# Layer 0 of a four-layer network: the position bias as three half-size Toeplitz products in place of four, and the residual copied to phase order by ScalarE

## The chip, the cores and the metric

The kernel runs on one core of a Trainium2 chip. Its time is the device time of one execution in microseconds (us); the figure compared is the median over runs. A profile is one execution of the same program taken by the hardware profiler. PE is TensorE's matmul, PEld its weight load, DVE is VectorE, ACT is ScalarE, POOL is GpSimd, SP is SyncE, which here only issues DMAs.

## What is computed

The input x is float32 of shape (T=4, B=8, N=512, D=512). Four layers follow one another, each of the form x = x + layer(groupnorm(x)). Layer 0 is a spiking attention; layers 1 to 3 are convolutions, which the change doesn't touch. Cut to what matters:

```python
# layer 0, on the group-normed x; lif() is a leaky neuron over the time axis T that gives 0/1 spikes
q = heads(lif(bn(x @ Wq.T)))          # H = 8 heads of 64
k = heads(lif(bn(x @ Wk.T)))
v = heads(lif(bn(x @ Wv.T)))
scores = einsum('tbhnd,tbhmd->tbhnm', q, k) / sqrt(D)
rel = pos[None, :] - pos[:, None] + (N - 1)
scores = scores + bias_table[rel].transpose(2, 0, 1)   # depends on m - n and the head alone
out = lif(einsum('tbhnm,tbhmd->tbhnd', scores, v))
out = lif(bn((out * gate_scale + gate_shift) @ Wp.T))
x = x + out
# layers 1 to 3: x = x + conv(groupnorm(x))
```

There is no softmax, so the attention falls into two linear parts: q (k^T v) / sqrt(D), and a product of v with a bias matrix that is Toeplitz (constant along its diagonals) for each head.

## The kernel before, in words

The program is written with a tile framework. It fixes the order of instructions on each engine when the program is built: a planner with its own estimates of durations takes the instructions in the order in which they are written as priorities, starts what it takes to be ready, and gives out the buffers. `tc.issue_after` adds an order by hand. On the chip each engine works through its list in that fixed order, and waits where its data or buffer is not there yet.

Layer 0 runs over 32 steps, a batch element b and a time t each (`steps`, t innermost). In one turn of the main loop stands, in this order:

- `attend` for step n: k^T v for pairs of heads (L540), masked to the diagonal blocks by DVE into kvb (L545); then for each of the four pairs of heads j the product of q with it into the PSUM tile pa (L552, one buffer), and the bias product into pb (L560, two buffers). The bias table is held as three bf16 parts (z) in the tiles `toep`, reversed so that a slice of 512 columns is the moving operand for a chunk c of 128 tokens. So a step has 4 pairs x 4 chunks x 3 parts x 2 heads = 96 matmuls of 512 columns. The two heads of a pair write the two halves of the PSUM partitions. DVE then adds pa and the neuron's state (L572; ScalarE does it for t = 0, L570), adds pb (L575), makes the spikes `so` (L469), and resets (L471); ScalarE halves the state (L473).
- `load_x` of the residual xr (SyncE, L438), from the pool `x0` of six buffers, shared with the loads xs for the statistics of the next group of batch elements (L456).
- `project_in` for step n + 1: v, k and q, each in four chunks of eight PE instructions (L524), their potentials and spikes on DVE (L485, L492, L529, L469, L499, L471), the states of v and k on GpSimd (L500), that of q on ScalarE (L475). vtok, k and q have one buffer each.
- Between those, `project_out` of step n: four chunks (L587). The potential v_p comes out in phase order (every fourth column together), as layer 1 wants it. DVE adds the spikes to the residual (L598, two instructions of 256 elements in a chunk, reading xr at a stride of four elements) into x1s, a tile with two buffers, and takes its statistics (L602). GpSimd copies mirrored edges (L609) and stores the tile (L614). ScalarE issues six DMAs for mirrored rows where the chunk is the first or the last (L617, L620).
- In between, DVE normalises the input of step n + 2 (L643) and transposes it in four pieces into xn (L505, six buffers), which all projections of that step read.

At the start the bias table is loaded, split in three parts by DVE and stored to DRAM (`split_bias`, L369 to L375). Then `prepare_bias` loads each pair of heads of each part as 128 shifted rows (hankel, L388; 2 x 896 columns, 448 KB) and ScalarE copies it reversed into `toep` (L394), twelve times.

Layer 1 (L843) and layers 2 and 3 (L1146, L1249) follow. Constants of the later layers (`same`, `ind`, `mask2`) are loaded with `block` in one DMA at the start (L142).

Of the kernel before, what the change touches and what calls it, by code (L numbers as in the profile page):

```python
# [129 lines left out]
def network(ctx: ExitStack, tc: tile.TileContext, i: dict, out: bass.AP):  # L130
# [9 lines left out]
    n_c = i["c128"].shape[1] - SHIFTS * M1  # L140
    c128 = const.tile([P, n_c], F32, name="c128")
    nc.gpsimd.dma_start(c128, i["c128"][:, :n_c])  # L142
    at = 0

    def part(n):
        nonlocal at
        at += n
        return c128[:, at - n : at]

    block, same, ind = part(P), part(P), part(G)  # L150
    mask2 = part(W2_N * 2)
# [8 lines left out]
    avg_same = const.tile([P, P], F32, name="avg_same")  # L160
# [49 lines left out]
    st1 = [const.tile([P, T, PAIR, NC, 2, 6], F32, name=f"st1_{g}") for g in range(G)]  # L210
# [20 lines left out]
    nc.vector.tensor_scalar_mul(avg_same, same, 1.0 / n_half)  # L231

# [3 lines left out]
    late = ctx.enter_context(pool("late", side="right"))  # L236
    st2 = late.tile([P, T, B, W1_N // 2 // N_PS1, 6], F32, name="st2")
# [30 lines left out]
def layer0(  # L268
# [22 lines left out]
    toep = [wpool.tile([P, H, NC * P + N - P], BF16, name=f"toep_{j}") for j in range(3)]  # L291
# [5 lines left out]
    xp = s.enter_context(tc.tile_pool(name="x0", bufs=6))  # L297
# [32 lines left out]
    def as_rows_of(cols):  # L330

        n = cols.shape[1]
        ps = ps_mm.tile([n, P], F32, tag="mm", name="ps_rows")
        nc.tensor.transpose(ps, cols, ident)
        rows = wpool.tile([4 * NC, P], F32, tag="rows", name="rows", bufs=2)
        nc.scalar.copy(rows[:n], ps)
        return rows[:n]
# [16 lines left out]

    def prepare_in(n):
# [6 lines left out]
    n_h, n_u = 2 * N - 1, toep[0].shape[2]  # L362

    def split_bias():

        n_e = n_h // 3
        parts = tc.dram_tile([3, H * n_h], BF16, name="bias_parts")
        src = state.tile([3 * H, n_e], F32, tag="h_o", name="bias_table")
        nc.scalar.dma_start(src, bass.AP(i["table"].tensor, 0, [[n_e, 3 * H], [1, n_e]]))  # L369
        part = state.tile([3 * H, 3, n_e], BF16, tag="h_p", name="bias_part")  # L370
        for z in range(3):
            nc.vector.tensor_copy(part[:, z, :], src)
            if z < 2:
                nc.vector.tensor_sub(src, src, part[:, z, :])
        nc.scalar.dma_start(  # L375
            bass.AP(parts.tensor, parts.offset, [[n_e, 3 * H], [H * n_h, 3], [1, n_e]]), part
        )
        return parts

    def prepare_bias(parts):  # L380


        for h in range(0, H, 2):
            for z in range(3):
                hankel = state.tile(
                    [P, 2, n_u], BF16, tag="h_o" if (h + z) % 2 else "h_p", name="hankel"
# [4 lines left out]
                        parts.tensor, parts.offset + (z * H + h) * n_h, [[1, P], [n_h, 2], [1, n_u]]  # L391
                    ),
                )
                nc.scalar.copy(toep[z][:, h : h + 2, :], hankel[:, :, ::-1])  # L394
# [6 lines left out]
    def prepare_out(wp32):  # L401
# [3 lines left out]
        for e in range(NC):  # L405
# [16 lines left out]
            c_twice["p"].rearrange("p (g v) -> p g v", g=PH), phases(along_free(as_rows_of(c), 0)), 2.0  # L422
        )
        for k in range(NC):
            wp = work.tile([P, D], F32, tag="v", name="wp_k", bufs=3)
            nc.vector.scalar_tensor_tensor(
                wp.rearrange("p (g v) -> p g v", g=PH), phases(wp32[:, k, :]),
# [14 lines left out]
    def load_quarters(b, t):  # L442
# [5 lines left out]
        return xt  # L448

# [52 lines left out]
    def transposed(xt, k):  # L502

        xk = work.tile([P, N], F32, tag="xn", name="xn", bufs=6)
# [28 lines left out]
    def attend(got, t):  # L533
# [13 lines left out]
        for j in range(NC):  # L547
            pa = ps_1.tile([P, N], F32, tag="pa", name="ps_a")
            pb = ps_b.tile([P, N], F32, tag="pb", name="ps_b")
            for two in range(2):  # L550
                out = slice(two * DH, (two + 1) * DH)
                nc.tensor.matmul(  # L552
                    pa[out, :], lhsT=kvb[:, j, out], rhs=q[:, j, :], start=True, stop=True
                )
            for c in range(NC):
                u = P * (NC - 1 - c)
                for z in range(3):
                    for two in range(2):
                        h = 2 * j + two
                        nc.tensor.matmul(  # L560
                            pb[two * DH : (two + 1) * DH, :],
                            lhsT=v[:, c, h * DH : (h + 1) * DH],
                            rhs=toep[z][:, h, u : u + N],
                            start=c == 0 and z == 0,
                            stop=c == NC - 1 and z == 2,
                        )
            h = h_of["o"][:, j, :]
            w = work.tile([P, N], F32, tag="v", name="v_o", bufs=3)
            if t == 0:
                nc.scalar.mul(w, pa, half_scale)  # L570
            else:
                nc.vector.scalar_tensor_tensor(  # L572
                    w, pa, half_scale, h, op0=ALU.mult, op1=ALU.add
                )
            nc.vector.scalar_tensor_tensor(w, pb, 0.5, w, op0=ALU.mult, op1=ALU.add)  # L575
# [3 lines left out]
    def project_out(so, c, xt, b, t):  # L579
# [12 lines left out]
        x1 = x1p.tile([P, PH, X1_U], F32, tag="x1", name=f"x1s_{b}_{t}_{c}")  # L592
        by_phase = xt.rearrange("p (v g) -> p g v", g=PH)
        for z in range(2):
            f, u = (2 * z + R1) % PH, (2 * z + R1) // PH
            own = x1[:, f : f + 2, u : u + NV]
            two = slice(2 * z, 2 * z + 2)
            nc.vector.scalar_tensor_tensor(  # L598
                own, v.rearrange("p (g v) -> p g v", g=PH)[:, two, :], 1.0,
# [748 lines left out]
```

## Time and profile before

| | us |
|---|---|
| median of 3 runs | 2902.83 |
| lowest, highest | 2902.46, 2903.03 |
| profiled execution, span of the core's instructions | 2900.8 |
| the same with what lies around the span | about 2902.8 |
| start until the first projection (L524) | 22.7 |
| layer 0's steps, up to | about 2024 |
| layer 1, from / layers 2 and 3, from | 2032 / 2490 |

The page of a profile gives each engine's busy time and share, the span in slices, the DMA queues, the chain of work that ended last (followed back from the last instruction, at each step to what released it), and the costliest groups of instructions. A group's line reads: source line, engine, operation, output tile <- input tiles, shapes, count, then busy time and mean ns of one, then the idle time of the engine just before and what ended it. The busy time counts overlapping instructions once, so two matmuls that run side by side add less than their sum. In a timeline each line gives start and length in us, engine, line and operation; a length runs to the end of the instruction's own pipeline, so that neighbours overlap a little. The mean granted clock of TensorE was 0.991 of full speed over the span, 1.00 in layer 0 after its start, 0.91 in the first 110 us.

### The profile page before, as it was taken

Reading aid. Unit: us, or ns where it says so; the run is one execution under the profiler, and the core shown is the slowest. Engines: PE = TensorE matmul, PEld = TensorE weight load, DVE = VectorE, ACT = ScalarE, POOL = GpSimd, SP = SyncE. Lnnn points to the kernel's source line nnn. Section 1 sums busy time; section 2 is a strip of 40 time slices with the busy share of each in tenths; the row PEclk is TensorE's granted clock in tenths of the full one; section 3 lists DMA queues with packets and bytes.
Section 4 is the critical chain, followed back from the end, with each engine's and each line's share of the span. In section 5 each row is a group of like instructions: output and inputs, shape, how many; then the busy total and the mean of one; then the engine's idle time right before and its main releaser. Section 6 shows DMA issues by size and latency. Waiting matters only on the chain. (4 is left out here: it accounts for less than half of the span.)

```text
span 2900.8 us, 36559 instructions
## 1 busy us (share of the span) xinstructions
PE 2818.8 (97%) x12868; PEld 1302.5 (45%) x12868; DVE 2183.1 (75%) x3888; ACT 549.2 (19%) x851; POOL 868.8 (30%) x1920
## 2 busy tenths in 40 slices
PE   7999999999999999999999999999999999689999
PEld 3444555545555545455555555445333333223334
DVE  6897788788779878878877886886665665888870
ACT  2200100011010001001000000110111121677774
POOL 2242243333234323333422343332311111232220
PEclk9899999999999999999999999999999999999999
DMA  8433222223222232222222122212877788699975
GB/s 209 115 89 76 59 67 67 74 74 74 59 67 67 77 76 68 59 67 67 75 67 51 45 59 52 52 45 75 221 203 207 209 219 224 157 201 234 224 191 148
DMA packets 326127, 324.01 MB, mean 112 GB/s; under 512 B 21519, under 2 KB 240439, under 8 KB 325831
## 3 DMA queue, kind: packets, MB, share of 16 engines
q1 hardware_dynamic: 263024, 239.48, 34.1%
q0 software_dynamic: 19776, 56.14, 6.0%
q10 hardware_dynamic: 43143, 26.05, 3.1%
q8 instruction: 101, 1.65, 0.3%
q14 instruction: 83, 0.68, 0.1%
HBM read 212.44 MB, written 103.65 MB: 109 GB/s over the span
## 5 line engine op out<-in xcount | busy, mean ns | idle before, releaser
L524 PE MATMUL ps_in<-w_v,xn 128*128 128x512 f32 x1024 | 459.1, 599 | 5.4 <-DVE w_v L359 5.4
L524 PE MATMUL ps_in<-w_kq,xn 128*128 128x512 f32 x1024 | 449.8, 592 | 0.0
L843 PE MATMUL ps_conv<-x,bt 112*64 112x512 f32 x2048 | 445.2, 592 | 0.1
L524 PE MATMUL ps_in<-xn,w_kq 128*128 128x512 f32 x1024 | 444.9, 592 | 0.0
L560 PE MATMUL ps_b<-toep,vtok 128*64 128x512 bf16 x3072 | 367.1, 383 | 0.4 <-DVE v_o L575 0.4
L475 ACT ACTIVATE h_q<-v_q,c_half 128x512 f32<-128x512 f32 x96 | 69.1, 721 | 1473.6 <-DVE v_q L471 893.9
L500 POOL TENSOR_TENSOR h_v<-h_v,c_v 128x512 f32<-128x512 f32 x96 | 121.8, 1269 | 728.0 <-DVE h_v L499 700.1
L587 PE MATMUL ps_out<-wp,so 128*128 128x512 f32 x1024 | 308.7, 444 | 0.0
L609 POOL COPY x1s<-x1s 128x2 f32<-128x2 f32 (+1 forms) x1024 | 226.6, 275 | 273.0 <-DVE x1s L598 273.0
L524 PEld LDWEIGHTS ps_in<-xn,w_kq 128*128 128x128 f32 x1024 | 194.3, 190 | 232.5 <-issue 220.4
L524 PEld LDWEIGHTS ps_in<-w_kq,xn 128*128 128x128 f32 x1024 | 194.3, 190 | 220.7 <-issue 206.2
L524 PEld LDWEIGHTS ps_in<-w_v,xn 128*128 128x128 f32 x1024 | 191.4, 191 | 222.9 <-issue 212.1
L843 PEld LDWEIGHTS ps_conv<-x,bt 112*64 112x64 f32 x2048 | 146.5, 135 | 288.0 <-issue 286.0
L560 PEld LDWEIGHTS <-vtok 128*64 128x64 bf16 x3072 | 176.1, 111 | 155.1 <-issue 5.6
L1249 PE MATMUL ps_conv<-x,band_t 64*64 64x512 f32 x2040 | 242.7, 595 | 0.0
L587 PEld LDWEIGHTS ps_out<-wp,so 128*128 128x128 f32 x1024 | 192.6, 188 | 94.0 <-issue 57.8
L1153 DVE SCALAR_TENSOR_TENSOR x<-ps_conv,inv,x 128x512 f32<-128x512 f32 (+1 forms) x172 | 186.1, 1169 | 46.9 <-PE ps_conv L1146 46.7
L598 DVE SCALAR_TENSOR_TENSOR x1s<-v_p,xr 128x256 f32<-128x256 f32 x256 | 187.6, 773 | 14.6 <-DMA x<-x1s 3.8
L865 POOL DMA_DIRECT2D x<-xo x128 | 71.4, 564 | 330.6 <-ACT xo L850 316.3
L850 ACT ACTIVATE xo<-ps_conv,off 128x512 f32<-128x512 f32 x128 | 87.6, 687 | 430.6 <-PE ps_conv L843 307.4
L500 POOL TENSOR_TENSOR h_k<-h_k,c_k 128x512 f32<-128x512 f32 x96 | 122.0, 1270 | 138.4 <-DVE h_k L499 138.4
L1146 PE MATMUL ps_conv<-xq,band 128*128 128x512 bf16 (+1 forms) x516 | 131.5, 391 | 31.3 <-POOL xq L1129 31.3
(193 smaller groups left out, 3113.8 us busy)
## 6 DMA issues: line engine op xcount, KB each, us to landing
x<-x SPq DMA_DIRECT2D x64, 917.0 KB
x<-x SPq DMA_DIRECT2D x168, 256.0 KB
x<-x1s POOLq DMA_DIRECT2D x128, 262.0 KB, 2.7
xq<-in_x SPq DMA_DIRECT2D x128, 256.0 KB
xr<-in_x SPq DMA_DIRECT2D x128, 256.0 KB
out<-o SPq DMA_DIRECT2D x164, 192.0 KB
xs<-in_x SPq DMA_DIRECT2D x112, 256.0 KB
x<-xo ACTq DMA_DIRECT2D x128, 128.0 KB
```

Source lines behind the costliest of these rows:

```text
L500: nc.gpsimd.tensor_add(h, h, c_twice[n])
L524: mm = nc.tensor.matmul(ps, lhsT=lhsT, rhs=rhs, start=k == 0, stop=k == NC - 1)
L560: nc.tensor.matmul(pb[two * DH : (two + 1) * DH, :], lhsT=v[:, c, h * DH : (h + 1) * DH], rhs=toep[z][:, h, u : u + N], start=c == 0 and z ...
L587: nc.tensor.matmul(ps, lhsT=so[:, k, c * P : (c + 1) * P], rhs=wpT[z][:, k, :], start=k == 0 and z == 0, stop=k == NC - 1 and z == 1,)
L598: nc.vector.scalar_tensor_tensor(own, v.rearrange("p (g v) -> p g v", g=PH)[:, two, :], 1.0, by_phase[:, two, :], op0=ALU.is_ge, op1=ALU.add,)
L609: nc.gpsimd.tensor_copy(x1[:, f, u : u + n], x1[:, fm, um - n + 1 : um + 1][:, ::-1])
L843: mm = nc.tensor.matmul(ps[q * M1 : (q + 1) * M1, :], lhsT=bt[:, z, :], rhs=xt[:, w0 : w0 + N_PS1, z : z + NV], start=z == 0, stop=z == SH ...
L850: nc.scalar.activation(xo[:, a, :], ps, AF.Identity, bias=off[:, t : t + 1])
L865: engine.dma_start(bass.AP(dst.tensor, dst.offset + (q * n_half * W1_OUT * B + b) * D + f * NV, [[B * D, W1_OUT], [W1_OUT * B * D, n_half] ...
L1146: mm = nc.tensor.matmul(ps[:n_p, :], lhsT=w["band2"][:n_p, j, dx, :n_p], rhs=xq[:, j, dx : dx + PH, :], start=dx == 0, stop=dx == 2,)
L1153: done["DVE"] = nc.vector.scalar_tensor_tensor(own.rearrange("p (v g) -> p g v", g=PH), by_phase(ps[:n_p, :]), w["inv"][:n_p], by_phase(x[ ...
L1249: mm = nc.tensor.matmul(ps[j][b * HALF : (b + 1) * HALF, :], lhsT=band[half, b, dx, :], rhs=x3[half, s0 + j, dx : dx + D], start=dx == 0, ...
```

## The change

The 512 x 512 bias matrix of a head is seen as four blocks of 256 x 256: T0 on the diagonal (both blocks are the same), T+ and T- off it. With v's halves a (first 256 tokens) and b (last 256), the first half of the output is T0 (a + b) + (T+ - T0) b, the second half T0 (a + b) + (T- - T0) a. Three half-size products stand in place of four.

- `toep` holds for each head three tables of 384 columns (x = 0: T0; 1 and 2: the two differences) for one of 896. The bias table is scaled by sqrt(D) when it is prepared, so that q's product and the difference products add up in one PSUM tile pb (with `start=False` for the later ones); pa holds 256 columns of T0 (a + b), which both halves of the output read. The matmuls: 4 pairs x 3 products x 2 chunks x 3 parts x 2 heads = 144 of 256 columns.
- GpSimd makes `both` = a + b, bf16, 128 x 1024 elements a step. Its tile takes the one buffer of k.
- Preparation: five loads of the table for one, a subtraction and a scaling more on DVE, three stores for one; each hankel load is 6 x 384 columns (576 KB), as is each ScalarE copy.
- The residual: after its load ScalarE copies it in phase order into x1s (two copies of 256 elements a chunk); DVE's L598 then adds the spikes in place, reading contiguously. The x1s tile is now taken when the residual is copied.
- Room: `x0` has four buffers for six, xn five for six; the statistics tiles st1 of groups 2 and 3 are those of groups 0 and 1; the constants of the later layers are loaded after layer 0; two small tiles share the place of kvb.

```diff
-    toep = [wpool.tile([P, H, NC * P + N - P], BF16, name=f"toep_{j}") for j in range(3)]
+    toep = [wpool.tile([P, H, 3, N // 2 + P], BF16, name=f"toep_{j}") for j in range(3)]
-    xp = s.enter_context(tc.tile_pool(name="x0", bufs=6))
+    xp = s.enter_context(tc.tile_pool(name="x0", bufs=4))
...
-        for z in range(3):
-            nc.vector.tensor_copy(part[:, z, :], src)
-            if z < 2:
-                nc.vector.tensor_sub(src, src, part[:, z, :])
+        for x, first in enumerate((1, 2, 0)):
+            cut = slice(x * H, (x + 1) * H)
+            nc.scalar.dma_start(own[cut], rows(first))
+            if x > 0:
+                nc.scalar.dma_start(same[cut], rows(1))
+        nc.vector.tensor_sub(own, own, same)
+        nc.vector.tensor_scalar_mul(own, own, math.sqrt(D))
...
+    def own_of(x1, z):
+        f, u = (2 * z + R1) % PH, (2 * z + R1) // PH
+        return x1[:, f : f + 2, u : u + NV]
+
+    def residual_of(b, t):
+        got = []
+        for c, xt in enumerate(load_x(b, t, "xr")):
+            x1 = x1p.tile([P, PH, X1_U], F32, tag="x1", name=f"x1s_{b}_{t}_{c}")
+            for z in range(2):
+                nc.scalar.copy(own_of(x1, z), phases(xt)[:, 2 * z : 2 * z + 2, :])
+            got.append(x1)
+        return got
...
-        xk = work.tile([P, N], F32, tag="xn", name="xn", bufs=6)
+        xk = work.tile([P, N], F32, tag="xn", name="xn", bufs=5)
...
-        for j in range(NC):
-            pa = ps_1.tile([P, N], F32, tag="pa", name="ps_a")
-            pb = ps_b.tile([P, N], F32, tag="pb", name="ps_b")
-            for two in range(2):
-                out = slice(two * DH, (two + 1) * DH)
-                nc.tensor.matmul(
-                    pa[out, :], lhsT=kvb[:, j, out], rhs=q[:, j, :], start=True, stop=True
-                )
-            for c in range(NC):
-                u = P * (NC - 1 - c)
+        both = work.tile([P, NC, D], BF16, tag="k", name="both")[:, :2, :]
+        nc.gpsimd.tensor_add(both, v[:, :2, :], v[:, 2:, :])
+        half = N // 2
+
+        def biased(out, own, j, x):
+            for c in range(2):
+                u = P * (1 - c)
                 for z in range(3):
                     for two in range(2):
                         h = 2 * j + two
                         nc.tensor.matmul(
-                            pb[two * DH : (two + 1) * DH, :],
-                            lhsT=v[:, c, h * DH : (h + 1) * DH],
-                            rhs=toep[z][:, h, u : u + N],
-                            start=c == 0 and z == 0,
-                            stop=c == NC - 1 and z == 2,
+                            out[two * DH : (two + 1) * DH, :],
+                            lhsT=own[:, c, h * DH : (h + 1) * DH],
+                            rhs=toep[z][:, h, x, u : u + half],
+                            start=x < 2 and c == 0 and z == 0, stop=x == 0 and c == 1 and z == 2,
+                            skip_group_check=x > 0,
                         )
+
+        for j in range(NC):
+            pa = ps_1.tile([P, half], F32, tag="pa", name="ps_a")
+            pb = ps_b.tile([P, N], F32, tag="pb", name="ps_b")
+            biased(pb[:, :half], v[:, 2:, :], j, 1)
+            biased(pb[:, half:], v[:, :2, :], j, 2)
+            for two in range(2):
+                out = slice(two * DH, (two + 1) * DH)
+                nc.tensor.matmul(
+                    pb[out, :], lhsT=kvb[:, j, out], rhs=q[:, j, :], start=False, stop=True,
+                    skip_group_check=True,
+                )
+            biased(pa, both, j, 0)
...
-            residual = load_x(b, t, "xr")
+            residual = residual_of(b, t)
```

## The prediction

> **What bounds the kernel now.** I read the page's engine line and its costliest groups first, then the busy time by stretches of the span, then the chain of work that ended last, then the timeline around one step's attention. The page says that TensorE is busy almost throughout, and in which lines:
>
> ```profile
> PE 2818.8 (97%) x12868; PEld 1302.5 (45%) x12868; DVE 2183.1 (75%) x3888; ACT 549.2 (19%) x851; POOL 868.8 (30%) x1920
> L560 PE MATMUL ps_b<-toep,vtok 128*64 128x512 bf16 x3072 | 367.1, 383 | 0.4 <-DVE v_o L575 0.4
> L598 DVE SCALAR_TENSOR_TENSOR x1s<-v_p,xr 128x256 f32<-128x256 f32 x256 | 187.6, 773 | 14.6 <-DMA x<-x1s 3.8
> ```
>
> An average says little about the stage that is changed, so here are 31 of layer 0's 32 steps, and one step alone (columns: stretch, then its length and the busy time of PE, PEld, DVE, ACT, POOL):
>
> ```profile
> 110.00:2024.00 1914.00, 1904.11 (x7739) 962.26 (x7740) 1540.74 (x2578) 140.29 (x212) 657.05 (x1413) 1.00 0.25 66
> 1903.00:1964.00 61.00, 60.89 (x248) 30.69 (x248) 55.19 (x82) 5.41 (x8) 25.12 (x48) 1.00 0.11 36
> ```
>
> PE idles 1914.00 - 1904.11 = 9.9 us there, 0.32 us a step. Layer 0 is PE-bound at full granted clock, and a column taken from PE is worth its whole time until something else is late. DVE is next: 55.2 of 61.0 us. The rates of PE come from the chain, where the numbers are start and length:
>
> ```profile
> 1955.12 2.59 PE ps_b L560 x24
> ...
> 2012.16 0.89 PE ps_kv L540 x16
> ...
> 2102.26 1.04 PE ps_band L951 x32
> ```
>
> 24 bias matmuls of 512 columns take 2.59 us: 107.9 ns each, since the two heads of a pair run side by side in the two column halves. 16 matmuls of 128 columns, each with its own weight load, take 55.6 ns each. 32 small ones in column halves, each with its weight load, take 32.5 ns. So a weight load and a matmul every 54 ns is within what PE does here. Last, the hand-over between the q projection and the attention, in PE's and in DVE's order, and an earlier moment of the same step:
>
> ```profile
> 1950.62 1.06 PE L540 MATMUL ps_kv<-vtok,k 128*128 128x128 bf16 x16
> 1951.61 1.05 PE L560 MATMUL ps_b<-toep,vtok 128*64 128x512 bf16 x8
> 1952.77 0.41 PE L552 MATMUL ps_a<-q,kvb 128*64 128x512 f16 x2
> ```
>
> ```profile
> 1950.91 0.75 DVE L485 SCALAR_TENSOR_TENSOR v_q<-ps_in,a_half,h_q 128x512 f32<-128x512 f32 x1 [0.49 <-PE ps_in L524]
> 1951.69 0.43 DVE L469 TENSOR_SCALAR q<-v_q 128x512 f16<-128x512 f32 x1
> 1952.03 0.68 DVE L545 TENSOR_TENSOR kvb<-ps_kv,c 128x512 f16<-128x512 f32 x1
> ```
>
> ```profile
> 1942.43 1.92 DVE L469 TENSOR_SCALAR q<-v_q 128x512 f16<-128x512 f32 x1
> ```
>
> ```profile
> 1942.78 1.28 POOL L500 TENSOR_TENSOR h_p<-h_p,c_p 128x512 f32<-128x512 f32 x1
> ```
>
> The planner filled the wait for kvb with eight bias matmuls; they end at 1951.61 + 8 x 0.108 = 1952.47, and PE then waits 0.30 us, to 1952.77, about all of a step's idle time. The last two rows show a price that I need: the q spikes, 0.43 us when undisturbed, took 1.92 us when GpSimd's add fell upon them.
>
> **What the Trainium skill says.** "SBUF — State Buffer", Who interferes with whom: VectorE and GpSimd share a port pair; a VectorE operation in a two-port mode and a GpSimd instruction exclude each other for their whole length, and a VectorE operation with two SBUF inputs excludes a GpSimd reader. The 1.92 us row agrees. "GPSIMD Engine Reference", 3.1 Elementwise: a two-input add costs about 2.6 cycles an element at 1.2 GHz[...]. This trace: 1.27 us for 512 elements (L500) and 0.19 us for a four-element copy (L1242), 2.1 ns an element; agrees. "TensorE: Matmul & The Clock Gate", Back-to-back issue gap: 262 cycles for 256 columns at 2.4 GHz, 109 ns. No matmul of 256 columns is in the trace; the 55.6 ns at 128 columns fits the same law.
>
> **The change, part by part.**
>
> *Products (L560).* Removed: 96 x 107.9 ns = 10.36 us a step. Added: four pairs of heads x three products x two chunks x three bf16 parts x two heads = 144 matmuls of 256 columns; a concurrent pair costs 109 ns, so 144 x 54.5 ns = 7.85 us. Saved 2.51 us a step, 80.3 us in 32. The q matmuls of L552 stay (0.22 us a pair, now into pb). Bounds: 54 to 56 ns each, 77 to 83 us.
>
> *The sum of the two halves of v, on GpSimd.* New, 1024 elements: 0.19 + 1024 x 2.1 ns = 2.35 us, taken as 2.4 (1.3 if bf16 ran twice as fast; 2.54 as two of L500). It takes k's only buffer, so it starts after the last kv matmul (1951.68, plus 0.11, the lag that L572 shows after L552: 1951.79). The q spikes hold the port until 1952.12; the add then ends near 1954.5, and PE gets it at 1954.6. PE meanwhile has 24 matmuls (1.31 us, to 1952.92; kvb is ready at 1952.7) and q's pair, to 1953.14. A gap of 1.46 us opens. Part can be filled: pb has two buffers, so the first two products of the next pair of heads (1.31 us) need nothing new, and the planner filled before. Bounds 0 and 1.5; I take 1.1 us: +35.2 us. The old 0.31 us is contained in it: -9.9. Behind the add on GpSimd nothing is urgent; behind DVE's L471, which also needs the port, stands the first L572, which comes later than that anyhow.
>
> *DVE in the attention.* A pair of heads costs DVE 0.69 + 0.68 + 0.42 + 0.69 = 2.48 us (L575, L572, L469, L471), PE so far 2.81, now 36 x 0.0545 + 0.22 = 2.18. DVE becomes the slower, by 0.3 us a pair, and pa, one buffer, holds PE. Bounds 0 (two pb buffers, spare work) and 4 x 0.3 = 1.2 us a step; I take 0.5, +16.0 us.
>
> *Residual.* L598 reads contiguously: about 0.41 us (a statistic of 256 elements, L602) for 0.77, some 90 us off DVE in all. It isn't what PE waits for outside the attention, so zero; it pays for the tail above. ScalarE gets 256 copies of 0.44 us (half of a 0.63 us L473 above a 0.25 us small copy) to 0.9 us if strided reads cost it as they do DVE; ScalarE is busy 140 of 1914 us. The third and fourth wait for the store of the first and second x1s: the first x1s of a step is at 1911.75, its store is issued at 1914.94 and lands 2.7 us later, the third is used at 1929.72. About 9 us of slack with two copies in it: zero. Queued behind a waiting copy are h_q and h_o (needed a step later) and, in eight steps, L570. If the cover went, L598 would stall DVE by the excess. Four x0 buffers for six delay SyncE's statistics loads; DVE waited 40.6 us for those in all, 1.9 at most, inside its slack: zero, up to 0.3 a step.
>
> *One xn buffer less.* One more transpose (0.70 us) must wait for the q projection's end, where DVE idles 0.49 us. Zero, bound 0.4 a step.
>
> *Start.* The bias chain on DVE (five operations, 7.75 to 9.87) gets half longer and two operations more, about +2 us ahead of the first projection, at 22.7. Each hankel load is 576 KB for 448, each ScalarE copy 2304 columns for 1792 (1.69 to 2.17 us): +5.8 us in twelve, and +1.6 MB at the 180 GB/s of this stretch, 9 us. The last copy ended at 88.8, the first attention at 104.1, which hides most. I take +5 in all; bounds 0 and 17.
>
> *The rest* (later load of masks, shared st1, halved buffers): behind a 13.9 us image of layer 1, zero, bound 3.
>
> Sum: -80.3 + 35.2 - 9.9 + 16.0 + 5.0 = -34.0. From the profiled execution's 2902.8 (span 2900.8 and some 2 us around it; the median of the runs is 2902.83 too): **2868 us**.
>
> **Rivals.** *Covered:* the planner puts the next pair's products under the add, as it put eight matmuls under kvb. Then no gap: 2834 us. For it: that row. Against: its times don't include the port. *The port, half lost:* the q spikes start at 1951.69, the add would start at 1951.79, a lead of 0.1 us that the extra transpose can eat. If the add is first, the spikes end near 1954.6, kvb at 1955.2, and PE, done at 1952.92, waits 2.35 us. In the 24 steps that carry state: 24 x 2.35 + 8 x 1.1 = 65 for 35: 2899 us. *Slower, the port lost in every step:* 32 x 2.35 = 75, and DVE's four pairs start late, so its tail costs 0.7: 22; start 10. -80.3 + 75 - 9.9 + 22 + 10 = +17: 2920 us. It decides above 2.51 + 0.31 - 0.16 (start) = 2.66 us of gap and tail a step. For it: the 1.92 us row and DVE's 90% load; against: in this step the spikes would be first.
>
> **How the numbers follow.** Forecast 0.48, covered 0.22, half lost 0.16, lost 0.14. Below 2897 (0.2%, about what a measurement of this kernel tells from no change) lie the first two and half of the third: faster 0.78, same 0.08, slower 0.14. The range from 2828 to 2908 leaves out the last and a little of the second's own spread.
>
> **What would show it.** Right: the bias matmuls at 54 to 56 ns each, a step of about 60 us for 61.4, one GpSimd add of 2.4 us a step, and PE waiting for it before each attention's first product of the sum. Covered: no such wait. Port lost: L469 of q at 2 us and more beside the add, PE waiting for kvb. DVE tail: PE waiting for L572. Wrong altogether: a pair of 256-column matmuls at over 0.12 us, or DVE standing before L598 for ScalarE's copies.

## The result, and the profile after

| | before | after |
|---|---|---|
| median, us | 2902.64 (4 runs) | 2966.40 (4 runs) |
| lowest, highest | 2902.36, 2903.03 | 2965.80, 2966.68 |
| ratio, 95% interval | | 1.0222 [1.0207, 1.0236] |
| profiled execution, span | 2900.8 | 2964.5 |
| mean granted clock of TensorE | 0.991 | 0.977 |

The change makes the kernel 64 us slower; the forecast was 34 us faster. Of the error of 98 us some 90 lie in one place, steps 1 to 22. The first k^T v product of each step marks where the step begins, and the marks give this table (us):

| | before | after | difference in all |
|---|---|---|---|
| first step begins at | 84.0 | 87.7 | +3.7 |
| step 0 | 71.1 | 78.7 | +7.6 |
| steps 1 to 22, mean | 62.04 | 64.91 | +63.2 |
| steps 23 to 30, mean | 61.51 | 60.31 | -9.6 |
| last step begins at | 2012.0 | 2076.9 | +64.9 |

From the last step's beginning to the end it is 888.8 us before and 887.6 after: layers 1 to 3 are unchanged. The forecast of -80.3 + 35.2 - 9.9 + 16.0 is -1.22 us a step. The last eight steps of the table come to nearly that, -1.20 (in part by luck, as shown below). What sets steps 1 to 22 apart is that another group of batch elements follows: they load images (xs) and take their statistics on VectorE. There a step became 2.87 us longer in the mean.

The lines that answer to those of before. First the engine line of the page of the changed kernel:

```profile
PE 2778.5 (94%) x14404; PEld 1406.8 (47%) x14404; DVE 2187.8 (74%) x3891; ACT 708.9 (24%) x1107; POOL 915.2 (31%) x1953
```

PE is busy 40 us less than before (2818.8), although the execution is 64 us longer: it waits. Then the groups of instructions of the changed kernel (busy us in all, mean ns of one, idle time before and what ended it):

```profile
L586 PE MATMUL ps_b<-toep,vtok 128*64 128x256 bf16 x3072 | 213.5, 294 | 1.3 <-DVE v_o L616 1.3
...
L474 ACT COPY x1s<-xr 128x256 f32<-128x256 f32 x256 | 156.8, 656 | 1094.1 <-DMA x<-x1s 1066.0 <-DVE xq L679 12.3 <-DVE h_v L527 11.9
...
L635 DVE SCALAR_TENSOR_TENSOR x1s<-v_p,x1s 128x256 f32<-128x256 f32 x256 | 135.7, 569 | 18.7 <-ACT x1s L474 6.5 <-DVE v_p L520 5.1 <-issue 1.1
...
L586 PE MATMUL ps_a<-toep,both 128*64 128x256 bf16 x1536 | 119.6, 297 | 14.0 <-POOL both L576 7.7 <-ACT v_o L611 5.9
...
L576 POOL TENSOR_TENSOR both<-vtok 128x1024 bf16<-128x1024 bf16 x32 | 70.4, 2201 | 239.8 <-PE ps_kv L568 239.8
```

ScalarE's copy takes 0.66 us, GpSimd's sum 2.20, and the residual's addition 0.57 for 0.77 before. PE waits for the sum only 7.7 us in the whole execution (8 times). The 1066 us that ScalarE waits ahead of its copies are no cost by themselves, but they say what the copies wait for: the store of an earlier x1s. Layer 0 as a stretch, and one of its last steps (columns as before):

```profile
110.00:2087.00 1977.00, 1872.54 (x9274) 1064.44 (x9275) 1550.72 (x2593) 292.78 (x465) 702.62 (x1444) 0.98 0.24 65
1776.00:1836.00 60.00, 59.18 (x299) 33.45 (x298) 44.02 (x72) 8.21 (x14) 16.44 (x41) 1.00 0.21 54
```

PE idles 1977.0 - 1872.5 = 104.5 us where it idled 9.9, and its clock there is 0.98, no longer 1.00. In the step of the second row it idles 0.8 us. The products themselves are as fast as forecast, by the chain of work that ended last in such a step (start and length):

```profile
1777.29 2.34 POOL both L576
...
1779.68 0.85 PE ps_a L586 x12
1780.52 1.31 PE ps_b L586 x24
```

24 matmuls in 1.31 us are 54.6 ns each. Now a step in the middle, number 5, around the hand-over from projections to attention (timeline: start, length, engine, line; in brackets the idle time before and what ended it):

```profile
416.99 0.69 DVE L484 BATCH_NORM_STATS2 st<-xs 128x6 f32<-128x512 f32 x1 [2.40 <-DMA xs<-in_x]
...
425.44 0.69 DVE L484 BATCH_NORM_STATS2 st<-xs 128x6 f32<-128x512 f32 x1 [0.27 <-DMA xs<-in_x]
...
428.81 0.69 DVE L484 BATCH_NORM_STATS2 st<-xs 128x6 f32<-128x512 f32 x1 [0.84 <-DMA xs<-in_x]
...
429.30 1.06 PE L568 MATMUL ps_kv<-vtok,k 128*128 128x128 bf16 x16
429.43 0.73 DVE L513 SCALAR_TENSOR_TENSOR v_q<-ps_in,a_half,h_q 128x512 f32<-128x512 f32 x1
...
430.29 1.50 PE L586 MATMUL ps_b<-toep,vtok 128*64 128x256 bf16 x24
430.44 2.16 POOL L576 TENSOR_TENSOR both<-vtok 128x1024 bf16<-128x1024 bf16 x1 [6.29 <-PE ps_kv L568]
430.54 0.70 DVE L533 STREAM_TRANSPOSE xn<-xq 128x512 f32<-128x512 f32 x1
431.16 1.98 DVE L499 SCALAR_TENSOR_TENSOR v_q<-v_q 128x512 f32<-128x512 f32 x1
433.07 1.29 DVE L533 STREAM_TRANSPOSE xn<-xq 128x512 f32<-128x512 f32 x2
...
434.29 0.70 DVE L513 SCALAR_TENSOR_TENSOR v_q<-ps_in,a_half,h_q 128x512 f32<-128x512 f32 x1
...
435.37 0.68 DVE L573 TENSOR_TENSOR kvb<-ps_kv,block 128x512 f16<-128x512 f32 x1
...
436.11 0.41 PE L601 MATMUL ps_b<-q,kvb 128*64 128x512 f16 x2 [4.32 <-DVE kvb L573]
```

PE ends its kv products at 430.36 and the 24 bias products behind them at 431.79, and then needs kvb. Behind the last statistic VectorE still has two q potentials, a reset of q that lasts 1.98 us (0.69 when undisturbed) while GpSimd's sum runs, and three transposes. It stands there late because three of the four statistics ahead of that waited for loads, 2.40 + 0.27 + 0.84 us: the last of them starts 0.5 us ahead of the kv products (428.81 for 429.30), in the same step of the kernel before 6.3 us (400.36 for 406.67). From the start of the last kv product to that of kvb it is 5.0 us in the mean of steps 1 to 22; before it was 0.87. From the lists of waits of the whole execution, before and after (us in all, times, longest):

```profile
DVE st L456 <- DMA xs<-in_x: 40.6, 60, 1.9
PE ps_a L552 <- DVE kvb L545: 10.5, 8, 2.9
```

```profile
DVE st L484 <- DMA xs<-in_x: 95.3, 66, 3.9
PE ps_b L601 <- DVE kvb L573: 94.8, 25, 6.1
```

PE's wait for kvb went from 10.5 to 94.8 us, which is 94.8 / 22 = 4.3 us a step if it is laid upon steps 1 to 22. That is not all of the cost. After a wait of this length PE runs at half its clock for a while (stretches of 2 us of step 5; the third number from the right is the granted clock):

```profile
434.00:436.00 2.00, 0.00 (x0) 0.00 (x0) 1.97 (x5) 0.00 (x0) 0.00 (x0) 1.00 0.15 44
436.00:438.00 2.00, 1.89 (x22) 1.57 (x24) 1.06 (x3) 0.72 (x1) 0.00 (x0) 0.68 1.15 236
438.00:440.00 2.00, 2.00 (x22) 1.67 (x20) 1.90 (x4) 0.00 (x0) 0.00 (x0) 0.50 1.25 196
```

The second group of 24 products took 2.77 us in that step for 1.48 in a step without a wait, and the step's bias products were busy 10.27 us for 8.77. So step 5 costs 4.3 us of wait and 1.5 of slow clock, less the 2.5 of saved products and 0.3 of old idle time of the forecast: +3.0. It lasts 64.75 us for 61.39 before, +3.4; the mean of the 22 is lower because the steps at t = 3 lose nothing (-0.3 to -0.8 us against before).

### The profile page after: what moved, and what is told of

The parts are those of the page before. It is cut to its first block, busy times and chain, and to the rows that moved or that the text cites. A ratio compares the mean times of both kernels' runs of the same rounds, so it can differ in the third digit from the quotient of the medians.

```text
span 2964.5 us, 40186 instructions
## 1 busy us (share of the span) xinstructions
PE 2778.5 (94%) x14404; PEld 1406.8 (47%) x14404; DVE 2187.8 (74%) x3891; ACT 708.9 (24%) x1107; POOL 915.2 (31%) x1953
## 5 line engine op out<-in xcount | busy, mean ns | idle before, releaser
L474 ACT COPY x1s<-xr 128x256 f32<-128x256 f32 x256 | 156.8, 656 | 1094.1 <-DMA x<-x1s 1066.0
L645 POOL COPY x1s<-x1s 128x2 f32<-128x2 f32 (+1 forms) x1024 | 200.1, 250 | 246.2 <-DVE x1s L635 243.1
L586 PE MATMUL ps_b<-toep,vtok 128*64 128x256 bf16 x3072 | 213.5, 294 | 1.3 <-DVE v_o L616 1.3
L887 ACT ACTIVATE xo<-ps_conv,off 128x512 f32<-128x512 f32 x128 | 87.7, 687 | 352.8 <-PE ps_conv L880 317.8
```

Of the source, the lines that this page charges most:

```text
L474: nc.scalar.copy(own_of(x1, z), phases(xt)[:, 2 * z : 2 * z + 2, :])
L586: nc.tensor.matmul(out[two * DH : (two + 1) * DH, :], lhsT=own[:, c, h * DH : (h + 1) * DH], rhs=toep[z][:, h, x, u : u + half], start=x < ...
L645: nc.gpsimd.tensor_copy(x1[:, f, u : u + n], x1[:, fm, um - n + 1 : um + 1][:, ::-1])
L887: nc.scalar.activation(xo[:, a, :], ps, AF.Identity, bias=off[:, t : t + 1])
```

## The experiments

Two theories stood at the start: **A**, the smaller buffer counts make VectorE late, and **B**, GpSimd's sum holds the port pair that VectorE needs. Differences below are to the kernel before on the same chip, in us; the changed kernel stands at +63.8. All but the last two were run once. The single executions of the kernel before beside them lie between 2898.9 and 2902.9 us, and those of one kernel in e17 and e18 up to 5 us apart, so differences of a few us say nothing.

| run | what it is | us | to before |
|---|---|---|---|
| e1 | before, x0 = 4, xn = 5 | 2916.9 | +14.0 |
| e2 | after, x0 = 6, xn = 6 | 2902.4 | -0.5 |
| e3 | after, no sum | 2928.0 | +25.1 |
| e4 | after, sum on VectorE | 2939.8 | +36.9 |
| e5 | after, x0 = 6 alone | 2915.1 | +16.3 |
| e6 | after, xn = 6 alone | 2951.4 | +52.6 |
| e7 | e2 without the sum | 2865.9 | -33.0 |
| e8 | after, statistics first in the program | 2963.5 | +64.6 |
| e9 | e8, residual loads held behind | 2964.1 | +62.8 |
| e10 | e9, sum on VectorE | 2939.2 | +37.9 |
| e11 | e10, two transposes behind kvb | 2917.8 | +16.4 |
| e12 | e2, residual as before | 2881.7 | -19.6 |
| e13 | e9, statistics behind kvb | 2896.1 | -6.8 |
| e14 | e13, sum on VectorE | 2855.7 | -47.2 |
| e15 | e14, two transposes behind kvb | 2855.7 | -47.2 |
| e16 | after, residual as before | 2897.9 | -5.0 |
| e17 | e14, timed | 2855.8 | ratio 0.9837 [0.9822, 0.9852] |
| e18 | e14, residual as before, timed | 2869.8 | ratio 0.9891 [0.9874, 0.9907] |

In e2, e5, e6, e7 and e12 the third bf16 part of the Toeplitz tables lies in the second's memory to make room, so the bias is computed with a wrong third part. In e3 and e7 the first half of v stands in for the sum, which then doesn't take k's buffer either. The other kernels compute the whole reference.

### Which part costs what: e1 to e4

```diff
 e1, on the kernel before
-    xp = s.enter_context(tc.tile_pool(name="x0", bufs=6))
+    xp = s.enter_context(tc.tile_pool(name="x0", bufs=4))
-        xk = work.tile([P, N], F32, tag="xn", name="xn", bufs=6)
+        xk = work.tile([P, N], F32, tag="xn", name="xn", bufs=5)
 e2, on the kernel after: the same two lines the other way, and
-    toep = [wpool.tile(... name=f"toep_{j}") for j in range(3)]
+    toep = [wpool.tile(... name=f"toep_{j}") for j in range(2)]
+    toep.append(toep[1])
 e3, on the kernel after
-        both = work.tile([P, NC, D], BF16, tag="k", name="both")[:, :2, :]
-        nc.gpsimd.tensor_add(both, v[:, :2, :], v[:, 2:, :])
+        both = v[:, :2, :]
 e4, on the kernel after
-        nc.gpsimd.tensor_add(both, v[:, :2, :], v[:, 2:, :])
+        nc.vector.tensor_add(both, v[:, :2, :], v[:, 2:, :])
```

> The kernel before with only two of the change's edits: x0 with four buffers for six, xn with five for six. Theory A (the smaller buffers make DVE late: statistics loads wait for x0, a third transpose stands ahead of the last q potential, so kvb is late and PE waits): slower by 25 to 60 us, PE waiting for kvb by 2 us and more in the steps that load statistics. Theory B (GpSimd's add holds the port pair and delays L499 and the spikes): within 5 us of the kernel before, since there is no add in it.

> The changed kernel with x0 at six and xn at six buffers again. The room comes from letting the third bf16 part of the bias share the second's tile, so the products use wrong third parts; their number and sizes are unchanged. Theory A: 2860 to 2890 us, the wait for kvb below 2.5 us in all steps. Theory B: 2940 us and more, the wait for kvb stays at 4 us, since the add still comes before the q spikes.

> The changed kernel without GpSimd's add: the third product reads the first half of v in place of the sum, so the sum of the halves is left out of the computation. Theory A: 2925 to 2950 us (1.3 us of L499's wait and the 1.2 us wait for the add go, the late statistics and transposes stay). Theory B: 2850 to 2880 us, the wait for kvb below 1 us nearly everywhere.

> The changed kernel with the sum of v's halves on VectorE in place of GpSimd (bf16, 1024 elements[...]). Theory A: 2930 to 2955 us, as without the add but with some more on DVE. Theory B: 2860 to 2890 us.

**e1: +14.0**, below what A expected and above B. The small buffers hurt the old kernel little, so they are no cause without the rest of the change. **e2: 64 us less than the changed kernel**, far more than B allows, but less than A expected (2860 to 2890), and PE still waits up to 6.0 us for kvb. **e3: 39 less, e4: 27 less**, as A expected; B had asked for 76 to 116. But A alone would leave the sum nearly free, and it isn't. Measured alone the two come to 64 + 39 = 103 us, and together (e7 below) to 97. Neither takes the kernel to the forecast.

### Each buffer, and both causes together: e5 to e7

```diff
 e5: e2, but                e6: e2, but
-  "x0", bufs=6             -  "x0", bufs=6
+  "x0", bufs=6             +  "x0", bufs=4
-  "xn", bufs=6             -  "xn", bufs=6
+  "xn", bufs=5             +  "xn", bufs=6
 e7: e2 with e3's edit
```

> The changed kernel with six x0 buffers again and xn left at five. Room is made by letting the third bf16 part of the Toeplitz tiles share the second's memory, so the third part's share of the bias is wrong; the instructions are the same. Both buffers together gave 2902.4, 64 us less than the changed kernel's 2966.4. Theory 'late statistics' (four x0 buffers make SyncE's statistics loads wait for ScalarE's copies of the residual, DVE gets them late, kvb stands behind them): most of the 64 comes back here, 2905 to 2930, and DVE's wait for these loads falls from 95 us to under 60. Theory 'transposes' (a third transpose stands ahead of the last q potential, because one xn buffer less keeps it from running earlier): little comes back, 2950 to 2966.

> The changed kernel with six xn buffers again and x0 left at four, with the same shared Toeplitz memory (wrong third part). 'Late statistics': 2940 to 2966, DVE's wait for the statistics loads stays at 80 us or more. 'Transposes': 2905 to 2930, two transposes instead of three around the end of the q projection and kvb earlier by 0.7 us or more a step.

> Both buffer counts restored (shared Toeplitz memory, third part wrong) and the sum of the two halves of v left out: the first half of v stands in for it, so one of three products is wrong. If buffers and add together are the whole cause, the products' saving of 80 us should now show: 32 steps of 59 to 60.5 us, 2835 to 2862 in all, and PE's wait for kvb under 1 us in nearly every step. If a third cause is there (DVE's order, ScalarE's copies, late residual loads in themselves), 2865 to 2890, with waits for kvb of 2 us and more left in the steps that carry statistics.

**e5 returns 47.5 us, e6 11.2** (differences to before, against +63.8): the buffers of the loads are the larger part, as 'late statistics' said. But one thing did not fit: VectorE's wait for the loads, which should have fallen below 60 us, was 90.8 in e5, in 42 waits for 66. The loads still came late. The statistics now stand further ahead of kvb, and still make it late: in step 6 of e5 the last of them starts 16.9 us ahead of the kv products (464.17 for 481.03), behind a wait of 3.67 us for a load, and kvb starts 5.2 us after the last of these products. **e7** gives 2865.9, above the 2835 to 2862 that 'the whole cause' had; its steps with statistics at t = 1 and 2, all but step 1, still wait 1.4 to 3.9 us for kvb. So a third cause was there. The steps without statistics show what the change can give: 58.6 to 59.4 us with PE never waiting, except where t = 0. There ScalarE, not VectorE, empties pa, and PE waits 0.84 us for it.

### When the loads are issued, and the copies: e8 to e12

```diff
 e8, on the kernel after
+            if n + 1 <= last:
+                next_group(n)
             residual = residual_of(b, t)
...
-            if n >= 0:
-                next_group(n)
 e9: e8, and, with the last statistics load on SyncE kept in loads["xs"]
-            residual = residual_of(b, t)
+            with tc.issue_after(loads["xs"]):
+                residual = residual_of(b, t)
 e10: e9 with e4's edit
 e11: e10, and for the transposes at the end of a turn, behind the next turn's attend
+            with tc.issue_after(done["kvb"]):
+                for k in range(2, NC):
+                    transpose(n + 1, k)
 e12: e2, with the residual's code of the kernel before
-            residual = residual_of(b, t)
+            residual = load_x(b, t, "xr")
```

> The changed kernel, complete and with its small buffers, but the next group's statistics are put ahead of the residual's loads in program order, so that their x0 slots come from the step before, and the residual loads wait instead. 'Late statistics': DVE's wait for the statistics loads falls below 50 us of 95, and the time falls by 25 to 60 us, to 2905 to 2940. 'Transposes' or 'port': 2955 to 2970. It can lose, if the residual's loads now wait for the statistics on DVE and ScalarE's copies come late to the stores: then x1s waits of DVE for ScalarE appear, and 2970 or more.

> The changed kernel, complete, with its small buffers; each step's statistics loads are held ahead of its residual loads on SyncE's queue (in the run before this one, program order alone did not move them: SyncE still issued two residual loads, the quarters and two more residual loads first). 'Late statistics': the loads land while the attention runs, DVE's wait for them falls from 95 us to under 20, and the time falls to 2895 to 2930 without any more memory. 'Port and transposes' alone: 2945 to 2966. If the residual loads come too late for ScalarE's copies, DVE waits at the first residual addition of a step and it ends above 2966.

> The same order of loads, and the sum of the halves of v on VectorE. The sum [...]freed 27 us when it was changed alone. If the two causes add: 2868 to 2905. If the waits for the loads hid the port's cost, so that both are the same microseconds: within 8 us of the run with the loads alone.

> The same again, and the last two transposes of each step are queued on VectorE behind kvb instead of ahead of the last q potential. 'Transposes': another 8 to 20 us, 2855 to 2890. Rival: the 1.4 us they take return as a later first potential of the attention, since VectorE is the slower engine there: within 5 us of the run without this edit, or slower.

> Six x0 and six xn buffers (third bf16 part shares the second's memory and is wrong), GpSimd's sum as in the changed kernel, and the residual as before: no copies on ScalarE, VectorE reads the loaded tile. The same with the copies took 2902.4. Theory 'copies': statistics loads wait on SyncE's queue for buffers that the copies hold back; without them 2880 to 2895, and DVE's wait for these loads falls from 86 us to 40 to 50. Theory 'copies are harmless': VectorE's addition costs 0.2 us more each, 2900 to 2915.

**e8 and e9 changed nothing** (+64.6 and +62.8), against my expectation of 25 to 70 us, and VectorE's wait for the loads stayed at 91.9 and 91.7 us. In e9 the residual's loads do stand behind the statistics' loads of the same turn. But those go out in the step before, in the places that its residual leaves, at about the same moment (for kv at 495.3: four from 480.69). Moving the queue entry doesn't help where the buffer isn't free. **e10** lies 25 us under e9, outside both of its ranges, since e9 had brought nothing: the sum's cost is apart from the loads. **e11** lies another 21 us lower: what stands between the q potentials and kvb counts while VectorE is late.

**e12: 2881.7, 19 less than e2** by the differences to before. The copies on ScalarE, priced at zero, cost that much although no computing engine waits much for them by name (VectorE waited 6.5 us for L474 in the changed kernel). VectorE's wait for the loads falls from 86 to 44.1 us. The SyncE queue of one step shows how, first before, then after (start, length of a whole group of issues):

```profile
448.86 10.43 SPq L438 DMA_DIRECT2D xs<-in_x  x4
460.82 1.88 SPq L438 DMA_DIRECT2D xr<-in_x  x2
```

```profile
462.47 8.52 SPq L451 DMA_DIRECT2D xr<-in_x  x2
479.32 12.25 SPq L451 DMA_DIRECT2D xs<-in_x  x4
```

Before, the last of the four is issued by 459.3, and the next kv products start at 468.1: 8.8 us later. After, it is issued by 491.6, and kv starts at 494.1: 2.5 us later. What these issues wait for stands in the changed kernel's waits of SyncE's queue and of ScalarE:

```profile
SPq L451 <- ACT x1s L474: 1262.4, 124, 25.5
```

```profile
ACT x1s L474 <- DMA x<-x1s: 1066.0, 117, 32.2
```

A load of the statistics needs a buffer of x0. That is given back by a copy on ScalarE, the copy needs one of two x1s tiles, and such a tile is free when a store has landed. In the kernel before these loads waited for VectorE's additions (L598, 999.9 us), and those hardly ever for a store (3.8 us). The four loads also follow one another through one buffer: ahead of step 6 each of the last three is issued 0.03 us after the statistic of the one ahead of it has ended, so that a late VectorE makes the next load late too. The first of them goes out 14.7 us ahead of the kv products, in the kernel before 19.2.

### The place of the statistics in VectorE's order: e13 to e16

Here I dropped 'late loads' as the cause for a sharper theory: late loads hurt only because VectorE works in order, and the statistics that wait for them are queued *in front of* the q potentials and kvb, though nobody needs them for long.

```diff
 e13: e9, and
-            if n + 1 <= last:
-                next_group(n)
+            if n + 1 <= last:
+                with tc.issue_after(done["kvb"]):
+                    next_group(n)
 e14: e13 with e4's edit          e15: e14 with e11's last edit
 e16: the kernel after, with the residual's code of the kernel before
```

> The changed kernel, complete, small buffers, GpSimd's sum. New theory 'order': VectorE runs its queue in order, and the planner put the four statistics of a loaded image just before kvb, counting on buffers that ScalarE's copies would free early; the copies wait for a store, so the loads land late and VectorE stands before them with the q potentials and kvb behind. Here the statistics are queued behind kvb and the loads ahead of the residual's. Then VectorE's wait for these loads, 95 us, falls below 15, kvb comes under 3 us after the last kv product in the steps with statistics, and the time is 2895 to 2925. Rival 'port': GpSimd's sum and the transposes alone make kvb late; 2945 to 2966. Second rival: the 2.4 us of statistics now make the attention late: 2930 to 2960, with PE waiting for VectorE at the second and third pair of heads.

> The same, with the sum of the halves of v on VectorE behind kvb. 'Order' and 'port' as two separate costs: another 15 to 35 us less than with the order alone. If the sum on VectorE now pushes the statistics and the attention back: within 10 us of it.

> The same with the sum on VectorE, and the last two transposes behind kvb as well. If the transposes ahead of the last q potential are the rest of kvb's lateness: 5 to 20 us less than the run without it, and no wait for kvb above 1 us in the steps with statistics. If VectorE's attention is then too full (statistics 2.4, transposes 1.4[...] on top of 9.9): slower than that run by 5 to 30.

> The changed kernel, complete, with small buffers and GpSimd's sum, but the residual as before: no copies on ScalarE. With large buffers this gave 2881.7 for 2902.4, 21 us less. Theory 'order': the copies' early release is what misled the planner, so here too 20 to 45 us come back, 2920 to 2945, and VectorE's wait for the statistics loads falls from 95 to 40 to 65 us. If four x0 buffers are the whole cause of late loads, the copies, which free them early, help: 2966 to 3000.

**e13: 2896.1, 70.5 us less than the changed kernel relative to before**, with its small buffers, its copies and its GpSimd sum all in place; the edit of e9 differs from it only in where the statistics stand, and e9 is 69.5 slower. The wait for the loads is gone from VectorE's list altogether, and PE's wait for kvb is 19.6 us for 94.8. But the place is not all that differs when it runs. Behind kvb the four statistics of a step follow one another without a wait (from 419.83 to 422.89 in the turn that starts at 415.9) and give their buffers back together, and the next four loads go out from 424.92 to 454.6, for statistics at 481.05 and later; in e9 they went out from 480.69 to 492.9 for kv products at 495.3. So e13 shows what the edit is worth, and doesn't part the later consumer from the earlier load. **e16: 68.8 us less**, by the other way: without the copies the loads come in time. One line of its VectorE waits:

```profile
DVE st L484 <- DMA xs<-in_x: 40.3, 55, 1.6
```

and the issue of four such loads on SyncE, for kv products at 475.1:

```profile
437.93 10.50 SPq L451 DMA_DIRECT2D xs<-in_x  x4
449.04 17.76 SPq L451 DMA_DIRECT2D xr<-in_x  x4
```

The wait is the 40.6 of the kernel before; the loads go out 27 us ahead of kv, the residual's behind them, on four buffers. e16 returned more than I had expected (20 to 45): with four buffers the copies cost 69 us, with six 19. So the copies, the x0 buffers and the order are three handles on one chain, and any one of them gives most of the loss back. What e13, e16 and e12 have in common is that VectorE waits no more for these loads than in the kernel before (0, 40.3 and 44.1 us for 40.6), where the changed kernel, e2, e5, e8 and e9 wait 86 to 95. **e14: 2855.7**, 40 us under e13, more than the 15 to 35 expected: the sum on GpSimd costs 1.26 us a step once VectorE isn't late. That is more than the 25 to 27 of e4 and e10, perhaps because the waits for loads hid part of it there, and near the 32.5 by which e7 lies under e2. **e15 equals e14**, against the 5 to 20 us expected: once VectorE isn't late, the transposes ahead of the last q potential cost nothing.

### The mended kernel, timed: e17 and e18

> The complete kernel of the fourteenth run, timed: statistics queued behind kvb, their loads ahead of the residual's, the sum on VectorE. One look gave 2855.7 against 2902.9 before. 'Order plus port' expects the same here: 2850 to 2862, ratio to before 0.982 to 0.986.

> That kernel with the residual as before, without ScalarE's copies. If the copies only do harm by misleading the order, and the order is now fixed by hand, they are harmless: within 6 us of the timed kernel beside it. If they cost something in themselves (waits of DVE, store order): 5 to 20 us less. If they relieve VectorE where it is late (the additions cost it 0.2 us more each without them): 5 to 15 us more.

**e17: 2855.77 against 2902.11 us, ratio 0.9837 [0.9822, 0.9852]**, a complete kernel, 46 us faster than the kernel before and 110 faster than the changed one. Its groups on VectorE:

```profile
L486 DVE BATCH_NORM_STATS2 st<-xs 128x6 f32<-128x512 f32 x112 | 72.6, 679 | 0.1
...
L501 DVE SCALAR_TENSOR_TENSOR v_q<-v_q 128x512 f32<-128x512 f32 x96 | 65.1, 679 | 1.6
...
L580 DVE TENSOR_TENSOR both<-vtok 128x1024 bf16<-128x1024 bf16 x32 | 21.8, 682 | 1.2 <-PE ps_kv L572 1.2
```

and layer 0 as a stretch:

```profile
110.00:1983.00 1873.00, 1851.60 (x9285) 1046.53 (x9282) 1558.31 (x2621) 287.93 (x465) 655.69 (x1418) 1.00 0.25 68
```

The statistics wait 0.1 us for their loads, the q resets last 679 ns where they were 835 in the changed kernel, and the sum takes 0.68 us instead of 2.20. PE idles 21.4 us at full clock. Steps 1 to 22 take 60.36 us, steps 23 to 30 59.49. **e18**, the same without ScalarE's copies, is 14 us slower than e17: with the order mended the copies are a gain, though they had cost 69 us without it. In the profiled executions 5 us of it arise by the end of step 1, and the rest in later steps, in some of which PE waits for kvb again.

## Why the prediction was wrong, step by step

- **Products, -80.3 us: right.** 54.6 ns each by the chain. The steps at t = 3 that wait for nothing go from 61.31 (before) to 58.59 us (e7), -2.72 for -2.51 a step.
- **The old idle time, 0.31 us a step: read wrongly.** It is a mean. The prediction's own line of one step (1903:1964) has 0.11 us of it, and PE's waits for kvb, 10.5 us before, are eight waits of 0.3 to 2.9 us, six of them in steps 0 to 22. The wait that was to grow was there already.
- **The sum on GpSimd, +35.2 - 9.9: right in size.** The sum took 2.20 us for 2.4 and starts 0.30 us after the last kv product starts. In the last steps, except at t = 0, PE waits 0.74 to 0.82 us for it, and they are 0.9 to 1.0 us longer than those of e7; the forecast was 1.1. Taken away (e7) or moved to VectorE (e14) it gives 32 to 40 us. The expected pair lines up: "SBUF — State Buffer", Who interferes with whom, of the Trainium skill says that a VectorE instruction with two inputs in SBUF, as this reset is, and a GpSimd instruction that reads SBUF get in each other's way; the reset of q at 1.98 us under the sum, 0.68 without it, agrees.
- **VectorE's tail in the attention, +16: not found in that form.** In a step of e7 without statistics PE is busy 58.80 of 58.80 us. Only t = 0 pays there, for ScalarE: about 1.2 us in eight steps, 10 us. So it is in part luck that the last eight steps of the changed kernel come so near to the forecast: at t = 1, 2 and 3 they are 1.7 to 1.8 us shorter than before, and at t = 0 they are 0.4 us longer, where PE waits 1.71 us for kvb and 0.92 for ScalarE.
- **Residual, zero: this failed, and with it the forecast.** It said "Four x0 buffers for six delay SyncE's statistics loads; DVE waited 40.6 us for those in all, 1.9 at most, inside its slack: zero, up to 0.3 a step." The runs showed 69 us (e16), 3.1 a step in 22 steps. Two things were missed. The slack was not looked for where it counts: the statistics stand ahead of kvb on an engine that works in order. In step 6 of the kernel before, the last of them starts at 461.65 and kvb at 469.47, and VectorE works without a break between the two, so there a later load is a later kvb by nearly its whole delay. And copies and buffers were costed apart, each inside the slack, although they follow one another in one chain of waits. The 9 us of slack that I had found for the third and fourth copy is that of the residual's addition; nobody asked who else waits for the buffer that the copy frees. The addition itself saves 0.20 us for the 0.36 taken (569 ns for 773): at its shortest it lasts 0.41 us, as forecast, but that was set against a mean, and the shortest before is 0.60.
- **One xn buffer, zero, bound 0.4 a step: the bound was nearly it.** 11 us (e6 against the changed kernel) to 17 (e2 against e5), 0.35 to 0.5 a step. It shows alone in the last steps at t = 0: with five buffers (the changed kernel, e5) PE waits 1.71 us for kvb there, with six (e6, e2) not at all. Once VectorE isn't late, moving two transposes behind kvb gains nothing (e15 against e14).
- **Start, +5: 11 us**, inside its bounds: 3.7 to the first step and 7.6 in step 0. But 104.1 was read wrongly as the first attention: it is the start of the next step's projections (L524). The first attention's bias products start at 79.59, ahead of the end of the last copy at 88.8, so that end was not hidden.
- **The slower rival: right side, wrong mechanism.** "The port, lost in every step" had a gap of 2.35 us and 2920 us. PE does wait for kvb, and the reset of q lasts 2 us beside the sum, but without the sum (e3) it is still 25 us slower than before. And none of my cases priced what an idle PE does afterwards. "TensorE: Matmul & The Clock Gate", What's actually happening, of the Trainium skill says that the array falls to half rate after an idle window of about 3.4 us; after the wait of 4.3 us the trace has 0.50, but in e2 2.1 us were enough once (last section). For the whole stretch PE was busy 1872.5 us in the changed kernel and 1851.6 in e17 for the same products: some 21 us of the 98 are slow clock.

**What stays open.** Why the order of VectorE has the statistics where it has them is argued, not shown: the planner would count on buffers that the copies free early, and doesn't know the store. The statistics behind kvb were not tried without the loads moved ahead. And no run keeps the loads late with the statistics behind kvb, so how much of e13's gain is the place of the statistics, and how much the earlier loads that came with it, is not shown.

## What to carry to other kernels

Ask of every wait on an in-order engine not how long it is on average, but what stands queued behind it: a transfer that nobody needs soon is still urgent if its consumer is queued ahead of the critical instruction, and a cheap mend, as here, can be to move that consumer. Where a change both takes buffers away and makes another engine responsible for freeing them, follow the chain buffer, copy, store to its end and price it once as a whole. When a change fails, try its parts with the obstacle removed: here the change gave 46 us once two edits of order and one of the engine were made.

## What the runs showed of the hardware that I had not expected

- Half clock is not tied to a fixed length of wait. In e2 a wait of 2.1 us was followed by 24 products in 2.77 us in one step, and a wait of about 2.2 us by full speed in the next. Over the waits for kvb of at least 1.5 us in steps 1 to 30 of all twenty traces, none of the 78 up to 1.95 us was followed by a granted clock of 0.50 within 6 us, 34 of the 51 from 1.98 to 3.51 us were, and all 107 from 3.59 us on.
- VectorE adds two bf16 tiles of 1024 elements in 0.68 us, and GpSimd takes 2.20. For one such sum beside a loaded VectorE the loaded engine was the better place: 40 us in 32 steps.
